# Value products of a windowed attention: both halves of the values side by side in 64 columns, the sums of the exponentials on VectorE, the division on GpSimd

## The chip, the cores and the metric

The kernel runs on one core of one Trainium2 chip. A core has five engines with a queue each[...]: TensorE (PE, with its weight loads shown as PEld), VectorE (DVE), ScalarE (ACT), GpSimd (POOL) and SyncE (SP), which here only issues transfers. What counts is the device time of one execution in microseconds; smaller is better. With one core there is no other core to wait for.

## The reference, cut to what matters

The program is one transformer block of the macaron kind on 4096 tokens of 256 features: half a mixture-of-experts feed-forward, then attention in windows of 64 tokens, then another half feed-forward with the same weights. The change touches the attention alone, and of it the softmax and the product with the values:

```python
xg = x.reshape(Bx, ng, LS, Cx)                 # windows of LS = 64 tokens, H = 16 heads of hd = 16
qkv = jnp.einsum('bglc,cd->bgld', xg, w_qkv)
q, k, v = jnp.split(qkv, 3, axis=-1)
...
att = jnp.einsum('bghqd,bghkd->bghqk', q, k) * scale
att = jnp.where(causal, att, -jnp.finfo(att.dtype).max)
att = jax.nn.softmax(att, axis=-1)
y = jnp.einsum('bghqk,bghkd->bghqd', att, v)
...
x = x + 0.5 * _L0_ffn_ref(_layernorm(x, axis=-1), ...)
x = x + _L0_attn_ref(_layernorm(x, axis=-1), ...)
x = x + 0.5 * _L0_ffn_ref(_layernorm(x, axis=-1), ...)
```

The feed-forward is a shared one (`silu(x @ sg) * (x @ su) @ sd`, 2048 wide) plus the two best of 8 experts for each token, each expert taking at most 640 tokens.

## The kernel before

Matrix products are made in fp16 with each operand split in a high part and a low part (the rounding error of the high one). A product of two split operands is three matmuls, high by high, high by low and low by high (`TERMS`, L35); a value that is already exact in one place needs two.

There are four phases (L747 to L785). In phase a the first shared feed-forward runs for half of the tokens while 32 tiles of 128 tokens are normalised and routed to the experts. Phase b is the first round of experts. In phase c the rest of the first shared feed-forward and most of the second one are the main work, and beside them 32 attention tiles of 128 tokens run. Phase d is the second round of experts and the last shared block. The change lies wholly in phase c.

Main work of phase c: `shared` (L345) handles a block of 512 tokens in 16 chunks of 128 hidden features. A chunk is `gate_up` (L292): six 128x512 matmuls for the gate into one PSUM tile `pgu`, a tanh on ACT (L309), a multiplication on DVE (L310), six matmuls for the up part into another `pgu`, a product on DVE (L315), the rounding to the high part `hh` on ACT (L317) and the low part `hl` on DVE (L318). Then `down` (L321) puts twelve 128x256 matmuls into the two accumulators `po`; it is deferred by one chunk, so that the PE has the next chunk's gate and up to do meanwhile. There are three PSUM buffers for `pgu`. One is free again when L310 or L315 has read it, so a late DVE instruction shows as a PE that waits for `DVE sl L310`. At the end of a block two more DVE instructions (L359) add the result to the residual.

Side work of phase c: `attn_tile` (L469) is a generator; each `yield` ends a step. `drive` (L673) lets the main work advance and gives the side work a share: with `RATE_C = 3` every live tile advances by one step for each chunk of the main work, and with `GAP_C = 4` a new tile starts every four chunks. So four tiles go with one block of 512 tokens, and within one chunk several tiles are at different steps: the tile that makes its maximum (L545) and copies its values (L550) stands beside its predecessor that makes its value products (L568).

The steps of a tile that matter here: the scores of 16 heads come from `psc` (L537, eight 128x64 matmuls for each of two windows `g`), and DVE adds the causal mask into `S`, [128, 16, 64] (L540). DVE takes the maximum over the keys (L545), POOL subtracts it (L546), and ACT copies the values `vs` into `V2` four times (L550). One step later ACT takes the exponential in place (L554) and rounds it to fp16 into `e16` (L556), and POOL makes the low part (L557). One step later a transposing DMA turns both into `ET`, [128, 16, 128], whose partitions hold high and low parts of the 64 keys. Two steps later come the value products:

- For every pair of heads the stationary operand is `ET` (128x128) and the moving one is 33 columns of `V2`: two heads' 16 features and a column of ones, whose product is the sum of the exponentials. There are two matmuls into the same columns of `py`, one for the high part of the values and one for the low part (L568, 32 matmuls a tile).
- DVE takes the reciprocal of the sums out of `py` (L571, once for each `g`), and multiplies `py` by it into `Y` (L574, twice for each `g`, 64 partitions each).

In the next step ACT rounds `Y` to fp16 (L162) and POOL makes the low part (L163); transposing DMAs, the output projection and the front of the second feed-forward follow (`front_steps`, L602; `stats`, L134, with its power on POOL, L142; `route`, L209; `scatter`, L275, with two indirect DMAs for each tile on POOL's queue, L283). For one tile out of four, POOL's queue has the scatters of a whole block of 512 tokens beside its attention work.

The order of the instructions on each engine's queue is fixed when the program is built. The builder goes by the order of the code and by a model of the time that each instruction takes (L821), so instructions of one engine that don't depend on each other may change places. [...]

```python
    with _tile.TileContext(nc, schedule_with_timeline_sim=True) as tc:
```

Of the kernel before, what the change touches and what calls it, by code (L numbers as in the profile page):

```python
# [8 lines left out]
F32 = mybir.dt.float32  # L9
F32R = mybir.dt.float32r  # L10
F16 = mybir.dt.float16
# [4 lines left out]
ALU = mybir.AluOpType  # L16
AX = mybir.AxisListType
# [3 lines left out]
P = 128  # L21
# [16 lines left out]
class Net:  # L38
# [395 lines left out]
    def attn_init(self, w_qkv, ln_w, w_proj):  # L434
        nc = self.nc
        a = self.at
        self.wqkv = a.tile([P, 2, 2, 3 * H], F16, name="wqkv")
        self.wpr = a.tile([P, 2, 2, H], F16, name="wpr")
        for k in range(2):
            for c0, n in ((0, 2 * H), (2 * H, H)):  # L440
                r = a.tile([P, 2 * H], F32, name="rq", tag="q32")[:, :n]
                nc.sync.dma_start(out=r, in_=w_qkv[k * P:(k + 1) * P, c0:c0 + n])
                self.split(self.wqkv[:, 0, k, c0:c0 + n], self.wqkv[:, 1, k, c0:c0 + n], r)
        wp = w_proj.rearrange("(j r c) f -> r j c f", r=2, c=16)
        for k in range(2):
            r = a.tile([P, H], F32, name="rp", tag="yy")
            for j in range(8):
                nc.sync.dma_start(out=r[j * 16:(j + 1) * 16], in_=wp[k, j])
            self.split(self.wpr[:, 0, k], self.wpr[:, 1, k], r)
        self.lnw = a.tile([P, H], F32, name="lnw")  # L450
        nc.sync.dma_start(out=self.lnw, in_=ln_w.unsqueeze(0).to_broadcast([P, H]))
        self.mask = a.tile([P, 64], F32, name="mask")
        m2 = self.sm.tile([P, 64], F32, name="m2", bufs=1)
        for m, base in ((self.mask, 0), (m2, -64)):
            nc.gpsimd.memset(m, 0.0)
            nc.gpsimd.affine_select(
                out=m, in_=m, pattern=[[-1, 64]], compare_op=ALU.is_ge, fill=-3.0e38,
                base=base, channel_multiplier=1)
        nc.vector.tensor_copy(self.mask[64:P], m2[64:P])
        self.QK = a.tile([P, 24, P], F16, name="QK")  # L460
        nc.gpsimd.memset(self.QK, 0.0)
        self.V2 = []
        for i in range(2):
            v = a.tile([P, 2, 2, 8, 34], F16, name=f"V2{i}")
            nc.gpsimd.memset(v[:, :, 0, :, 32:33], 1.0)
            nc.gpsimd.memset(v[:, :, 1, :, 32:33], 0.0)
            self.V2.append(v)

    def attn_tile(self, R, j, x2, new_fb):  # L469

        nc = self.nc
        a = self.at
# [11 lines left out]
        V2 = self.V2[j % 2]  # L484
# [8 lines left out]
        for i in range(2):  # L493
            nc.scalar.activation(qk[:, i, :], pqk[:, i, :], AF.Square, scale=1.0 / XP, accum_out=ss[:, i:i + 1])
        nc.vector.tensor_scalar(
            out=ss, in0=ss, scalar1=XP ** 2 / H, scalar2=1e-6 * XP ** 2, op0=ALU.mult, op1=ALU.add)
# [6 lines left out]
            out=vs[:, 1, :], in0=pv, scalar=1.0 / XP, in1=vs[:, 0, :], op0=ALU.mult, op1=ALU.subtract)  # L503
        yield
        yield
        for i in range(2):
            nc.vector.scalar_tensor_tensor(
                out=qk[:, i, :], in0=pqk[:, i, :], scalar=ss[:, i:i + 1], in1=self.lnw,
                op0=ALU.mult, op1=ALU.mult)
        QS = self.QK[:, 0:16].rearrange("p (j s) (r a c) -> p j s r a c", s=2, r=2, a=4)  # L510
        for i in range(2):
            if i == 0:
                for r in range(2):
# [5 lines left out]
                        out=s[:, :, 2:4, :], in0=src, in1=s[:, :, 0:2, :], op=ALU.subtract)  # L519
            else:  # L520
# [4 lines left out]
                    out=s[:, :, 1::2, :], in0=src, in1=s[:, :, 0::2, :], op=ALU.subtract)  # L525
        yield
        QT = a.tile([P, 2, 24, 64], F16, name="QT")
        for g in range(2):
            nc.sync.dma_start_transpose(
                out=QT[:, g], in_=self.QK[g * 64:(g + 1) * 64].rearrange("p j c -> p (j c)"))  # L530
        yield
        yield
        S = a.tile([P, 16, 64], F32, name="S")
        for g in range(2):
            p = self.m1([P, 8, 64], F32, "psc")
            for jj in range(8):
                nc.tensor.matmul(  # L537
                    p[:, jj, :], lhsT=QT[:, g, 2 * jj:2 * jj + 2, :].rearrange("p r q -> p (r q)"),
                    rhs=QT[:, g, 16 + jj, :], start=True, stop=True)
            nc.vector.tensor_tensor(  # L540
                out=S[:, g * 8:(g + 1) * 8, :], in0=p,
                in1=self.mask.unsqueeze(1).to_broadcast([P, 8, 64]), op=ALU.add)
# [4 lines left out]
            out=S, in0=S, in1=mx.unsqueeze(2).to_broadcast([P, 16, 64]), op=ALU.subtract)  # L547
        for g in range(2):
            for d in range(2):
                nc.scalar.copy(  # L550
                    V2[d * 64:(d + 1) * 64, g, :, :, 0:32],
                    vs[g * 64:(g + 1) * 64].rearrange("p l (j c) -> p l j c", c=32))
        yield
        nc.scalar.activation(S, S, AF.Exp, scale=0.25)  # L554
        e16 = a.tile([P, 16, 2, 64], F16, name="e16")
        nc.scalar.copy(e16[:, :, 0, :], S)  # L556
        self.anchor = nc.gpsimd.tensor_tensor(out=e16[:, :, 1, :], in0=S, in1=e16[:, :, 0, :], op=ALU.subtract)  # L557
        yield
        ET = a.tile([P, 16, P], F16, name="ET")
# [2 lines left out]
        yield  # L562
        Y = a.tile([P, 2, 8, 16], F32, name="Y", tag="yy")
        for g in range(2):
            py = self.m1([P, 8, 33], F32, "py")
            for jj in range(8):
                for l in range(2):
                    nc.tensor.matmul(  # L568
                        py[:, jj, :], lhsT=ET[:, g * 8 + jj, :], rhs=V2[:, g, l, jj, 0:33], start=(l == 0), stop=(l == 1))
            rc = self.sm.tile([P, 8], F32, name="rc")  # L570
            nc.vector.reciprocal(rc, py[:, :, 32])  # L571
            for r in range(2):
                sl = slice(r * 64, (r + 1) * 64)
                nc.vector.tensor_tensor(  # L574
                    out=Y[sl, g], in0=py[sl, :, r * 16:(r + 1) * 16],
                    in1=rc[sl].unsqueeze(2).to_broadcast([64, 8, 16]), op=ALU.mult)
        yield
        y = self.tok.tile([P, H], F32, name="y")
        nc.sync.dma_start(out=y, in_=R["acc"][j * P:(j + 1) * P])
# [246 lines left out]
```

## Time and profile before

| what | us |
|---|---|
| median of 3 runs | 1846.73 (1844.07 to 1847.13) |
| the profiled execution, its own time | 1844.18 |
| its span, first to last instruction | 1842.5 |
| first and last value product (L568) | 698.3 and 1317.8 |

| engine | 1020 to 1080 us, busy of 60.00 us | whole span, busy |
|---|---|---|
| PE | 59.34 | 1782.8 |
| DVE | 48.85 | 1204.9 |
| ACT | 40.03 | 952.2 |
| POOL | 40.69 | 769.5 |

The stretch from 1020 to 1080 us lies in the middle of phase c. A busy share tells how loaded an engine is and not which one sets the time; for that one looks at the few places where the PE waits, and follows the chain of releases back from there. The granted TensorE clock was 0.999 of full speed over the span, so the clock plays no part.

### The profile page before, as it was taken

To read this page: it belongs to the slowest core of one execution; us is meant where nothing else is said; L and a number is where in the kernel's file an instruction comes from. 1 tells how busy PE (TensorE), PEld (TensorE's weight loads), DVE (VectorE), ACT (ScalarE), POOL (GpSimd) and SP (SyncE) were. 2 spreads that over 40 slices of the span, in tenths; PEclk is the share of its full clock that TensorE was granted. 3 is DMA by queue.
4 is the path that set the end of the run, shared out by engine and by line. 5 is a ranking of instruction groups with operands and counts; after the bars stand their busy time and mean duration, and the time that the engine had idled before them with its cause. 6 is when DMAs were issued, how large, how long until landed. Compare 5 with 4: busy or idle time off the path is not lost.

```text
span 1842.5 us, 37619 instructions
## 1 busy us (share of the span) xinstructions
PE 1782.8 (97%) x13722; PEld 1197.0 (65%) x13722; DVE 1204.9 (65%) x2869; ACT 952.2 (52%) x2055; POOL 769.5 (42%) x1104
## 2 busy tenths in 40 slices
PE   6989999999999899999999999999999999999999
PEld 3545656777777556666666666666665677777765
DVE  7665545666666567787877878787755565666643
ACT  5333324555555365766666666666333455555542
POOL 7776540111221244567667676776530011112210
PEclk9999999999999999999999999999999999999999
DMA  9753022445554246767585776757213044455420
GB/s 291 224 142 94 12 63 69 107 107 114 128 115 101 58 80 110 118 114 158 104 148 117 140 137 119 152 98 125 48 30 87 27 111 111 108 112 127 104 47 12
DMA packets 447514, 196.61 MB, mean 107 GB/s; under 512 B 302369, under 2 KB 444381, under 8 KB 447264
## 3 DMA queue, kind: packets, MB, share of 16 engines
q1 hardware_dynamic: 429664, 173.03, 42.7%
q0 software_dynamic: 17664, 21.17, 6.7%
q8 instruction: 107, 1.75, 0.4%
q14 instruction: 79, 0.65, 0.1%
HBM read 81.04 MB, written 52.85 MB: 73 GB/s over the span
## 4 chain that ended last, share of the span: by engine, by line
PE 57%; POOL 12%; issue 11%; DVE 10%; DMA 5%; ACT 4%; SPq 1%; POOLq 0%; DVEq 0%; another core or an unknown queue 0%; ACTq 0%
PE pgu L302 36%; PE po L326 18%; POOL xg L283 3%; DVE sl L315 2%; DVE sl L310 1%; POOL X L281 1%; DVE hl L318 1%; POOL rstd L142 1%; POOL S L546 1%; DMA y<-in_L_attn_x_dram 1%; ACT hh L317 1%; PE pqk L599 1%; ACT sl L309 1%; POOL e L557 1%; DMA xg<-X,di 1%
## 5 line engine op out<-in xcount | busy, mean ns | idle before, releaser
L302 PE MATMUL pgu<-xb,sgu 128*128 128x512 f16 x3072 | 743.5, 380 | 20.3 <-DVE sl L310 8.0
L317 ACT CAST hh<-sl 128x512 f16<-128x512 f32 (+2 forms) x512 | 272.9, 533 | 485.4 <-DVE sl L315 471.4
L302 PE MATMUL pgu<-xe,wc 128*128 128x384 f16 (+1 forms) x3072 | 497.0, 299 | 0.8
L302 PEld LDWEIGHTS <-sgu 128*128 128x128 f16 x3072 | 294.0, 98 | 295.7 <-issue 29.6
L315 DVE SCALAR_TENSOR_TENSOR sl<-pgu,sl 128x512 f32<-128x512 f32 (+2 forms) x512 | 300.6, 587 | 215.5 <-PE pgu L302 180.1
L318 DVE TENSOR_TENSOR hl<-sl,hh 128x512 f16<-128x512 f32 (+2 forms) x512 | 311.0, 608 | 160.1 <-ACT hh L317 153.3
L326 PEld LDWEIGHTS <-hh 128*128 128x128 f16 x3328 | 319.8, 98 | 114.9 <-ACT hh L317 13.9
L302 PEld LDWEIGHTS <-wc 128*128 128x128 f16 x3072 | 300.5, 98 | 94.1 <-issue 1.9
L326 PE MATMUL po<-sdw,hh 128*128 128x256 f16 x2048 | 349.9, 273 | 10.1 <-ACT hh L317 6.8
L326 PE MATMUL po<-sdw,hl 128*128 128x256 f16 x1024 | 247.5, 273 | 11.7 <-DVE hl L318 10.4
L326 PE MATMUL po<-wd,hh 128*128 128x256 f16 x1280 | 223.6, 273 | 0.0
L326 PEld LDWEIGHTS <-hl 128*128 128x128 f16 x1664 | 162.8, 98 | 57.2 <-DVE hl L318 23.3
L422 POOL DMA_INDIRECT out_dram<-eo,eid x40 | 64.1, 1604 | 314.3 <-DVE hl L318 244.9
L313 ACT ACTIVATE sl<-pgu 128x384 f32<-128x384 f32 (+1 forms) x336 | 158.9, 473 | 56.7 <-PE pgu L302 27.6
L422 POOL DMA_INDIRECT acc<-eo,eid x40 | 64.8, 1621 | 266.2 <-DVE hl L318 227.4
L283 POOL DMA_INDIRECT xg<-X,di x128 | 131.3, 1026 | 66.2 <-issue 27.5
L326 PE MATMUL po<-wd,hl 128*128 128x256 f16 x640 | 152.5, 273 | 2.1 <-DVE hl L318 1.9
L310 DVE SCALAR_TENSOR_TENSOR sl<-sl,pgu 128x512 f32<-128x512 f32 x176 | 120.0, 682 | 45.4 <-ACT sl L309 43.2
L309 ACT ACTIVATE sl<-pgu 128x512 f32<-128x512 f32 x176 | 104.3, 593 | 42.3 <-PE pgu L302 36.3
L102 ACT ACTIVATE wc<-re 128x512 f16<-128x512 f32 x128 | 80.5, 629 | 78.0 <-PE pgu L302 51.2
L103 DVE SCALAR_TENSOR_TENSOR wc<-re,wc 128x512 f16<-128x512 f32 x128 | 88.3, 690 | 25.9 <-ACT wc L102 25.7
L546 POOL TENSOR_TENSOR S<-S,amx 128x1024 f32<-128x1024 f32 x32 | 62.1, 1939 | 79.1 <-DVE amx L545 72.1
(141 smaller groups left out, 1740.6 us busy)
## 6 DMA issues: line engine op xcount, KB each, us to landing
re<-in_L_ffn_rg_dram SPq DMA_DIRECT2D x128, 128.0 KB
re<-in_L_ffn_ru_dram SPq DMA_DIRECT2D x128, 128.0 KB
re<-in_L_ffn_rd_dram SPq DMA_DIRECT2D x128, 128.0 KB
xg<-zero SPq DMA_DIRECT2D x16, 650.0 KB
y<-acc SPq DMA_DIRECT2D x64, 128.0 KB
y<-in_L_attn_x_dram SPq DMA_DIRECT2D x32, 128.0 KB
acc<-xr SPq DMA_DIRECT2D x16, 256.0 KB
out_dram<-xr SPq DMA_DIRECT2D x16, 256.0 KB
```

The source lines that it names most:

```text
L103: nc.vector.scalar_tensor_tensor(out=lo, in0=src, scalar=WS, in1=hi, op0=ALU.mult, op1=ALU.subtract)
L283: i = nc.gpsimd.indirect_dma_start(out=R["xg"][:, :], out_offset=bass.IndirectOffsetOnAxis(ap=di[:, t, k:k + 1], axis=0), in_=X, in_offset ...
L302: nc.tensor.matmul(p, lhsT=wc[:, w, i, k, :], rhs=x[:, 2 * a + k, :], start=(j == 0), stop=(j == 5))
L309: nc.scalar.activation(s, p, AF.Tanh, scale=0.5 / XP)
L310: nc.vector.scalar_tensor_tensor(out=s, in0=s, scalar=1.0, in1=p, op0=ALU.add, op1=ALU.mult)
L313: nc.scalar.activation(s, p, AF.Silu, scale=1.0 / XP)
L315: nc.vector.scalar_tensor_tensor(out=s, in0=ps[1], scalar=1.0 / XP / (2.0 * XP if tanh else 1.0), in1=s, op0=ALU.mult, op1=ALU.mult)
L317: nc.scalar.copy(h[0], s)
L318: nc.vector.tensor_tensor(out=h[1], in0=s, in1=h[0], op=ALU.subtract)
L326: nc.tensor.matmul(o, lhsT=h[a][:, t * P:(t + 1) * P], rhs=wd[:, w], start=(c == 0 and j == 0 and t % 2 == 0), stop=(c == nch - 1 and j == 2),
L422: i = nc.gpsimd.indirect_dma_start(out=R["acc"][:, :], out_offset=bass.IndirectOffsetOnAxis(ap=ids[:, t:t + 1], axis=0), in_=eo, in_offset ...
L546: self.anchor = nc.gpsimd.tensor_tensor(out=S, in0=S, in1=mx.unsqueeze(2).to_broadcast([P, 16, 64]), op=ALU.subtract)
```

## The change

`V2` becomes [128, 2, 8, 2, 32]: for each pair of heads the high part's 32 columns and the low part's 32 columns lie side by side, and the column of ones is gone. One matmul with 64 moving columns takes the place of the two with 33. The sums of the exponentials come from a new reduction of `S` on VectorE (128 partitions, 16 heads of 64 keys), made in the step of the exponential, with one reciprocal for all 16 heads. VectorE adds the high and the low product out of `py`, a reduction over two elements, twice for each `g`. GpSimd then multiplies `Y` in place by the reciprocal, once for each `g`. The exponential that is summed is the fp32 one, where before it was the sum of its two fp16 parts.

```diff
-            v = a.tile([P, 2, 2, 8, 34], F16, name=f"V2{i}")
-            nc.gpsimd.memset(v[:, :, 0, :, 32:33], 1.0)
-            nc.gpsimd.memset(v[:, :, 1, :, 32:33], 0.0)
-            self.V2.append(v)
+            self.V2.append(a.tile([P, 2, 8, 2, 32], F16, name=f"V2{i}"))
...
-                    V2[d * 64:(d + 1) * 64, g, :, :, 0:32],
+                    V2[d * 64:(d + 1) * 64, g].rearrange("p j l c -> p l j c"),
                     vs[g * 64:(g + 1) * 64].rearrange("p l (j c) -> p l j c", c=32))
         yield
         nc.scalar.activation(S, S, AF.Exp, scale=0.25)
         e16 = a.tile([P, 16, 2, 64], F16, name="e16")
         nc.scalar.copy(e16[:, :, 0, :], S)
+        rc = self.sm.tile([P, 16], F32, name="rc")
+        nc.vector.tensor_reduce(out=rc, in_=S, axis=AX.X, op=ALU.add)
+        nc.vector.reciprocal(rc, rc)
         self.anchor = nc.gpsimd.tensor_tensor(out=e16[:, :, 1, :], in0=S, in1=e16[:, :, 0, :], op=ALU.subtract)
...
-            py = self.m1([P, 8, 33], F32, "py")
+            py = self.m1([P, 8, 2, 32], F32, "py")
             for jj in range(8):
-                for l in range(2):
-                    nc.tensor.matmul(
-                        py[:, jj, :], lhsT=ET[:, g * 8 + jj, :], rhs=V2[:, g, l, jj, 0:33], start=(l == 0), stop=(l == 1))
-            rc = self.sm.tile([P, 8], F32, name="rc")
-            nc.vector.reciprocal(rc, py[:, :, 32])
+                nc.tensor.matmul(
+                    py[:, jj].rearrange("p l c -> p (l c)"), lhsT=ET[:, g * 8 + jj, :],
+                    rhs=V2[:, g, jj].rearrange("p l c -> p (l c)"), start=True, stop=True)
             for r in range(2):
                 sl = slice(r * 64, (r + 1) * 64)
-                nc.vector.tensor_tensor(
-                    out=Y[sl, g], in0=py[sl, :, r * 16:(r + 1) * 16],
-                    in1=rc[sl].unsqueeze(2).to_broadcast([64, 8, 16]), op=ALU.mult)
+                cs = slice(r * 16, (r + 1) * 16)
+                nc.vector.tensor_reduce(
+                    out=Y[sl, g], in_=py[sl, :, :, cs].rearrange("p j l c -> p j c l"), axis=AX.X, op=ALU.add)
+            nc.gpsimd.tensor_tensor(
+                out=Y[:, g], in0=Y[:, g], in1=rc[:, g * 8:(g + 1) * 8].unsqueeze(2).to_broadcast([P, 8, 16]),
+                op=ALU.mult)
```

## The prediction

> **What bounds the kernel now.** I read the page first, then the groups of instructions between 660 and 1325 us with shapes kept apart, then the PE's timeline for its waits, then the chain of waits, and last the timelines of POOL and DVE. The page:
>
> ```profile
> span 1842.5 us, 37619 instructions
> PE 1782.8 (97%) x13722; PEld 1197.0 (65%) x13722; DVE 1204.9 (65%) x2869; ACT 952.2 (52%) x2055; POOL 769.5 (42%) x1104
> ```
>
> The PE is busy 97% of the span, which says that saved PE work could pay, not that it does. The durations of the operations that the change removes, or that are the nearest rows to what it adds (columns: line, engine, operation, tile, shapes, count, then busy us and mean ns of one):
>
> ```profile
> L568 PE MATMUL py<-V,ET 128*128 128x33 f16 x1024 | 31.1, 177 | 0.0
> L537 PE MATMUL psc<-QT 128*128 128x64 f16 x512 | 28.4, 193 | 0.0
> L571 DVE RECIPROCAL rc<-py 128x8 f32<-128x8 f32 x64 | 10.0, 184 | 2.1 <-remote 1.8
> L574 DVE TENSOR_TENSOR Y<-py,rc 64x128 f32<-64x128 f32 x128 | 36.6, 286 | 1.6
> L545 DVE TENSOR_REDUCE amx<-S 128x16 f32<-128x1024 f32 x32 | 38.8, 1211 | 0.1
> L518 POOL TENSOR_TENSOR QK<-qk,QK 128x256 f16<-128x256 f32 x62 | 41.0, 682 | 11.4 <-ACT QK L517 11.4
> ```
>
> The last row is the nearest to the new POOL work: 682 ns for 256 elements a partition. Matmuls overlap, so 177 and 193 ns are not what one costs. The chain of waits, between 690 and 760 us, has their pace (start, us, what):
>
> ```profile
> 714.22 0.47 PE psc L537 x16
> 738.07 0.80 PE py L568 x32
> ```
>
> 0.80/32 is 25.0 ns for a matmul of 33 columns, 0.47/16 is 29.4 ns for one of 64. Next, where the PE waits in the middle of phase c (its timeline; in brackets the idle time ahead and what ended it):
>
> ```profile
> 1017.47 1.46 PE L302 MATMUL pgu<-xb,sgu 128*128 128x512 f16 x6 [0.87 <-DVE sl L310]
> 1018.76 0.96 PE L568 MATMUL py<-V,ET 128*128 128x33 f16 x32
> 1019.57 0.38 PE L326 MATMUL po<-sdw,hh 128*128 128x256 f16 x2
> 1020.66 0.28 PE L326 MATMUL po<-sdw,hl 128*128 128x256 f16 x1 [0.71 <-DVE hl L318]
> ```
>
> This pair of waits comes back at 855.69, 936.79, 1098.16, 1178.86 and 1259.56 us: six times, once in 80.7 us, which is one block of 512 tokens with four attention tiles. Between them the PE runs without a gap (but 0.26 us at 918). So each of these six blocks ends with the PE waiting for DVE, and the PE alone isn't the bound. The chain of waits from 995 to 1080 us tells where the late DVE instruction comes from:
>
> ```profile
> 1041.56 1.29 PE pgu L302 x6
> 1043.04 0.90 issue
> 1043.94 0.39 ACT yp L162
> 1044.33 0.50 ACT sl L309
> 1044.85 0.69 DVE sl L310
> ...
> 1047.00 1.04 DVE dl L226
> 1048.41 0.55 POOL rstd L142
> ...
> 1059.16 1.13 DVE amx L545
> ```
>
> From 1042.85 (the end of the first piece) to the wait at 1098.16, which is 55.3 us, no PE work is on it: it goes through ACT, DVE and POOL. After 1066.5 it is mostly POOL, whose queue holds the scatters of the block (its timeline, in the last of the four tiles):
>
> ```profile
> 1083.80 1.10 POOL L283 DMA_INDIRECT xg<-X,di  x1 [0.31 <-issue]
> 1084.90 1.93 POOL L546 TENSOR_TENSOR S<-S,amx 128x1024 f32<-128x1024 f32 x1
> 1087.00 0.99 POOL L283 DMA_INDIRECT xg<-X,di  x1 [0.17 <-POOL S L546]
> ```
>
> POOL has no wait over 0.32 us between 1066.5 and 1093.1. So two things are within 1.6 us of each other in 80.7: the PE's own work, and a chain over the three other engines, and the longer is the chain.
>
> [...] 1211 ns for 1024 elements and 205 ns for 64 (L259) make 1.05 ns an element and 138 ns fixed; no row shows a reduction out of PSUM. [...] hl (L318, two SBUF inputs) takes 689 ns on average between 60 and 660 us and 760 ns in phase c, where POOL works beside it.
>
> **The change part by part, for one tile.**
>
> PE: 32 matmuls at 25.0 ns go and 16 at 29.4 come, 0.80 - 0.47 = -0.33 us. Over 32 tiles 10.6 us, if the PE sets the time throughout.
>
> DVE, the value step: two reciprocals of 0.20 and four multiplications that follow at 0.30 (1.20 for the four) go, 1.6 us. Four reductions of 64x256 into 64x128 come: 138 + 256 x 1.05 = 0.41 us each by the reduction row, 0.34 from start to start, since independent DVE instructions overlap by 0.08 (the 1.21 us of L545 is followed after 1.13). That is 1.4 to 1.6 us. [...] PSUM with the stride of 32 could add, and I bound it at twice, 3.2. I take 1.5: no change here. DVE adds no wait, it still waits for py.
>
> DVE, the exponential step, all new: a reduction just like L545 (1.13 us to the next instruction) and a reciprocal of 128x16 (0.20, as L571), 1.33 us. It waits for the exponential on ACT, and behind it in DVE's queue are that chunk's L310, L315 and L318, for which the PE's `pgu` buffers wait. Four tiles of a block, four places. (1) At 1024.87, the exponential's end, DVE is idle for 0.82 us and the PE is ahead on its own: hidden. (2) At 1044.04 DVE is idle until y (L592, 1044.34) and L310 at 1044.85; the reduction runs 1044.1 to 1045.2 and pushes a stretch that has no gap until 1048.4, where POOL's rstd (1048.41) waits for its end. With the gap used up, 0.95 us is left, on the chain. It stays there: POOL is then without a gap up to its ss at 1053.66, and DVE from 1054.4 to 1060.3. (3) At 1064.59 DVE is full too, but what follows on the chain is POOL, which gets to its rstd at 1072.27 while DVE has delivered the input (L140) at 1069.5: 2.8 us of cover, so hidden. (4) At 1087.93 the same: L140 ends at 1089.5, rstd starts at 1092.01. Without the cover each costs up to 1.33.
>
> POOL, all new: two multiplications of 128x128. From 682 ns at 256 elements and 1902 at 1024 (L546) it is 1.59 ns an element and 0.28 fixed, so 0.48 us each; start to start POOL's rows overlap by 0.06, so 0.42. Bounds: 0.2 (its smallest rows, L215) and 0.68. For tiles 1 to 3 POOL is waiting anyway around its yp (idle 1.46, 2.87 and 2.72 us ahead of it). In tile 4 it isn't: 0.84 us, all on the chain. Four memsets (L465, L466), 3.1 us of POOL at 630 us, go; the chain there is a scatter's DMA and weight loads, so nothing.
>
> ACT: the V2 copies have the same 64x512 elements, 0.62 us each. The rounding of Y (L162) now waits for POOL instead of DVE. Behind it in ACT's queue is the tanh (L309), for which L310 and the PE wait. For tiles 1 and 2 the multiplication is done in time, as L162 stands behind the exponential there. In tile 4 it isn't sure: at 1002.68 L162 starts as soon as Y is there, but POOL is in its scatters and in S until 1006.15. If the multiplication is queued behind S, L162 starts at 1007.0 and the tanh moves from 1002.99 to 1007.4; the up matmuls at 1006.2 need that chunk's L310, which then ends at 1008.7. A PE stall of 2.5 us, of which the 0.87 + 0.95 + 0.84 that the PE waits at the block's end anyway would take most: 0 to 2.5 us. I take 0.
>
> Sum for one of the six blocks: +0.95 + 0.84, and of the PE's gain only the one product that lies in the PE's part of the chain (1039.44), -0.33: +1.46. The saved PE time of the other products makes the wait at the block's end longer, that is what is late next: L310 behind POOL. Six blocks: +8.8. The other 8 tiles (before 830 and after 1263 us, where the chain is PE work or the PE has no such wait): 8 x -0.33 = -2.6. Together +6.2, from 1844.2 to 1850.4 for the profiled execution; its 1844.18 is 2.6 below the median of 1846.73, so 1852.9 against that.
>
> **The rivals.** *B, the whole PE gain:* the order of each queue is made anew when the program is built, and the reduction and the divisions may fall in gaps; the waits at the ends of blocks stay at 1.6 us. 10.6 off, 1836. For it: PE busy 59.34 of 60, DVE has 11 us of 60 idle. Against: with PE work gone, nothing shortens the POOL stretch. It decides if added DVE and POOL work costs the chain under 0.3 us a block. *C, everything added is hidden, and the gain goes into the wait at the block's end:* (8 + 6) x 0.33 = 4.6, 1842. Against it: POOL's stretch from 1066 to 1093. *D, queues behind a waiting head:* forecast plus the 2.5 us of tile 4 undiminished, 6 x 2.5 = 15 more: 1868. For it: ACT already idles 2.54 us at 1006.18 behind POOL's S. Against it: the overlap with the wait at the block's end.
>
> **How the numbers follow.** Forecast 0.42 (1853), B 0.22, C 0.16, D 0.20. The range takes B's centre and D's: 1836 to 1868, which leaves half of each, 0.2, outside. 0.2% is 3.7 us, about what a measurement of this kernel can tell from no change. Faster: B, 0.10 of C, 0.02 of the forecast where tile 2's reduction finds a gap: 0.34. Slower: D and 0.26 of the forecast: 0.46. The rest, 0.20, within.
>
> **What would show it.** PE: L568 with 512 matmuls, 0.47 us for 16. DVE: L545's twin at 1.21 us, the reductions out of py near 0.41. The wait of the PE for L310 at the end of each block grows from 0.87 to about 3, and the period from 80.7 to 82. If the period falls to 79.4, B is right; if tanh stands behind yp while POOL is in S, D. I am wrong if the blocks' order of instructions changes so that the POOL stretch isn't ahead of the PE's wait, or if a reduction out of PSUM costs far over 0.41.

## The result and the profile after

The changed kernel takes 1855.38 us (median of 7 runs, 1850.58 to 1859.45) against 1846.73 before (7 runs, 1844.07 to 1851.62). The ratio is 1.0047, with a 95% interval of 1.0032 to 1.0063: slower, by about 9 us. The profiled execution took 1859.45 us, with a span of 1857.7; it is the slowest of the seven, so the traces are compared by their periods and not by their ends. Line numbers are from here on those of each run's own kernel: the subtraction of the maximum on GpSimd is L546 before and L543 after.

The page of the changed kernel, busy times and shares of the chain of waits, and under it the second of these lines for the kernel before:

```profile
PE 1781.0 (96%) x13210; PEld 1188.3 (64%) x13210; DVE 1271.9 (68%) x2869; ACT 944.9 (51%) x2055; POOL 803.6 (43%) x1164
...
PE 59%; DVE 15%; issue 9%; DMA 5%; POOL 5%; ACT 5%; SPq 1%; another core or an unknown queue 0%; DVEq 0%; POOLq 0%; ACTq 0%
```

```profile
PE 57%; POOL 12%; issue 11%; DVE 10%; DMA 5%; ACT 4%; SPq 1%; POOLq 0%; DVEq 0%; another core or an unknown queue 0%; ACTq 0%
```

VectorE (DVE) is 67 us busier than before, GpSimd (POOL) 34. On the chain VectorE has gone from 10% to 15%, and GpSimd from 12% to 5%, although GpSimd has more to do: what the end hangs on has moved to VectorE. The groups of the changed kernel between 660 and 1355 us (line, engine, operation, tile, shapes, count, busy us, mean ns of one, idle time ahead):

```profile
L573 DVE TENSOR_REDUCE Y<-py 64x128 f32<-64x256 f32 x128 | 53.7, 419 | 1.8
L555 DVE TENSOR_REDUCE rc<-S 128x16 f32<-128x1024 f32 x32 | 38.8, 1212 | 6.3 <-ACT S L551 6.0
L575 POOL TENSOR_TENSOR Y<-Y,rc 128x128 f32<-128x128 f32 x64 | 27.8, 444 | 23.6 <-DVE Y L573 22.7 <-DMA QT<-QK 0.8
L567 PE MATMUL py<-V,ET 128*128 128x64 f16 x512 | 21.9, 193 | 0.0
L556 DVE RECIPROCAL rc<-rc 128x16 f32<-128x16 f32 x32 | 7.7, 241 | 0.1
```

The new instructions have about the lengths that were expected. Two old ones have not kept theirs. They are hl (L318), the low part of the feed-forward's hidden features, and nm (L150), minus the mean times the inverse deviation of each token, made twice for each tile. Both in the middle of phase c (840 to 1260 us), before and then after:

```profile
L318 DVE TENSOR_TENSOR hl<-sl,hh 128x512 f16<-128x512 f32 x83 | 61.1, 736 | 18.5 <-ACT hh L317 15.7 <-ACT S L554 1.4
L150 DVE SCALAR_TENSOR_TENSOR nm<-amv,arstd 128x1 f32<-128x1 f32 x21 | 3.2, 154 | 2.2 <-POOL arstd L142 2.2
```

```profile
L318 DVE TENSOR_TENSOR hl<-sl,hh 128x512 f16<-128x512 f32 x81 | 70.7, 873 | 17.5 <-ACT hh L317 13.7 <-issue 3.8
L150 DVE SCALAR_TENSOR_TENSOR nm<-amv,arstd 128x1 f32<-128x1 f32 x20 | 16.0, 798 | 1.6 <-POOL arstd L142 1.1
```

So hl takes 873 ns on average where it took 736, and one of the two nm, which has a single element a partition, 798 ns instead of 154. The waits of the PE in one block of the changed kernel:

```profile
1014.69 0.28 PE L326 MATMUL po<-sdw,hl 128*128 128x256 f16 x1 [0.84 <-DVE hl L318]
1020.84 0.61 PE L326 MATMUL po<-sdw,hh 128*128 128x256 f16 x4 [1.41 <-ACT hh L317]
1024.57 1.45 PE L302 MATMUL pgu<-xb,sgu 128*128 128x512 f16 x6 [0.72 <-DVE sl L310]
1042.74 0.39 PE L326 MATMUL po<-sdw,hh 128*128 128x256 f16 x2 [0.93 <-ACT hh L317]
1043.96 0.28 PE L326 MATMUL po<-sdw,hl 128*128 128x256 f16 x1 [0.82 <-DVE hl L318]
```

Where the PE waited 1.58 us in a block of 80.69 us, it now waits 4.7 us in this block and 4.3 in the median one, of 82.9 us (a block is counted from one POOL subtraction of S to the fourth after it). Its busy time in a block has fallen from 79.1 to 78.5 us, which is less than the 1.3 us that four tiles at 0.33 would give; where the rest went the trace doesn't show.

The timelines show why old instructions have grown. First VectorE, then GpSimd, in the changed kernel:

```profile
1017.18 2.16 DVE L150 SCALAR_TENSOR_TENSOR nm<-amv,arstd 128x1 f32<-128x1 f32 x1
...
1034.59 1.91 DVE L318 TENSOR_TENSOR hl<-sl,hh 128x512 f16<-128x512 f32 x1
```

```profile
1017.20 2.11 POOL L557 TENSOR_TENSOR e<-S,e 128x1024 f16<-128x1024 f32 x1
...
1033.82 2.13 POOL L557 TENSOR_TENSOR e<-S,e 128x1024 f16<-128x1024 f32 x1 [0.27 <-ACT e L553]
```

The GpSimd instruction beside both is e, the low part of the exponentials. The nm with one element ends when e ends (1019.34 and 1019.31). The hl begins 0.77 us into its e and ends 0.55 us after it (1036.50 and 1035.95). Both VectorE instructions have two tensor inputs in SBUF. From 840 to 1260 us, 26 of the 81 hl took over 0.73 us, up to 2.94, and each of the 26 ended 0.54 to 0.61 us after a GpSimd instruction did. The products sl (L310, L315) have as many elements, but one of their inputs is in PSUM: of these 163, 42 began inside a GpSimd instruction that wrote e, S, QK, yp, X, xa or Y and had up to 1.6 us left, and none took over 0.693 us. Nor did any of the new reductions of S, with one SBUF input, take over 1.221 us; 5 of the 20 began inside one, with up to 0.6 us left. Two inputs in SBUF aren't the whole of it, as ss (L492), with one tensor input, once took 0.66 us where 0.15 is its median, and ended 0.03 us after a GpSimd instruction. So the traces show VectorE instructions held until a GpSimd instruction ends; by what, they don't show. For nm and e they don't tell which began first either, as the two records start 0.02 us apart. While VectorE stands there, what is queued behind it stands too: L315, the next after this nm, starts at 1019.26.

### The profile page after: what moved, and what is told of

It is laid out like the page before. It is cut to its first block, busy times and chain, and to the rows that moved or that the text cites. A ratio compares the mean times of both kernels' runs of the same rounds, so it can differ in the third digit from the quotient of the medians.

```text
span 1857.7 us, 36680 instructions
## 1 busy us (share of the span) xinstructions
PE 1781.0 (96%) x13210; PEld 1188.3 (64%) x13210; DVE 1271.9 (68%) x2869; ACT 944.9 (51%) x2055; POOL 803.6 (43%) x1164
## 4 chain that ended last, share of the span: by engine, by line
PE 59%; DVE 15%; issue 9%; DMA 5%; POOL 5%; ACT 5%; SPq 1%; another core or an unknown queue 0%; DVEq 0%; POOLq 0%; ACTq 0%
PE pgu L302 37%; PE po L326 19%; DVE hl L318 3%; DVE sl L315 2%; DVE sl L310 2%; ACT hh L317 1%; POOL xg L283 1%; DVE Y L573 1%; PE pqk L600 1%; DMA xg<-X,di 1%; ACT V L547 1%; DVE nm L150 1%; DVE rc L555 1%; DMA xb<-X 1%; DVE st L137 1%
## 5 line engine op out<-in xcount | busy, mean ns | idle before, releaser
L315 DVE SCALAR_TENSOR_TENSOR sl<-pgu,sl 128x512 f32<-128x512 f32 (+2 forms) x512 | 300.3, 587 | 209.8 <-PE pgu L302 179.3
L318 DVE TENSOR_TENSOR hl<-sl,hh 128x512 f16<-128x512 f32 (+2 forms) x512 | 322.8, 631 | 149.6 <-ACT hh L317 141.5
L310 DVE SCALAR_TENSOR_TENSOR sl<-sl,pgu 128x512 f32<-128x512 f32 x176 | 119.0, 676 | 35.2 <-ACT sl L309 34.1
L543 POOL TENSOR_TENSOR S<-S,amx 128x1024 f32<-128x1024 f32 x32 | 62.1, 1940 | 74.6 <-DVE amx L542 74.6
```

The source lines that it names most:

```text
L310: nc.vector.scalar_tensor_tensor(out=s, in0=s, scalar=1.0, in1=p, op0=ALU.add, op1=ALU.mult)
L315: nc.vector.scalar_tensor_tensor(out=s, in0=ps[1], scalar=1.0 / XP / (2.0 * XP if tanh else 1.0), in1=s, op0=ALU.mult, op1=ALU.mult)
L318: nc.vector.tensor_tensor(out=h[1], in0=s, in1=h[0], op=ALU.subtract)
```

## The experiments

Three theories were set against each other. *VectorE work*: the reductions as such fill its queue. *GpSimd*: the divisions lengthen its stretch with the scatters. *Port*: the lost time is VectorE instructions with two SBUF inputs waiting for a GpSimd instruction to end. Port is only its name in the expectations; no run shows where the two engines meet. A fourth says that the builder only put the queues in a worse *order*. Every edit makes the builder order all queues anew, so one small ratio alone proves little. Ratios are to executions of the kernel before that were made beside each run, with 95% intervals. Names that start with a_ are edits of the changed kernel, those with b_ edits of the kernel before.

| run | ratio | interval | median us | block us | hl ns |
|---|---|---|---|---|---|
| before | 1 | | 1842.83 to 1844.40 beside these runs | 80.69 | 736 |
| the change | 1.0047 | 1.0032 to 1.0063 | 1855.38 | 82.89 | 873 |
| a_nosum | 1.0014 | 1.0007 to 1.0020 | 1846.28 | 81.74 | 918 |
| a_nodiv | 0.9991 | 0.9982 to 0.9999 | 1841.97 | 80.71 | 795 |
| a_neither | 0.9964 | 0.9950 to 0.9978 | 1838.04 | 80.30 | 882 |
| b_halfpe | 0.9932 | 0.9915 to 0.9949 | 1831.43 | 79.30 | 733 |
| b_plus_sum | 1.0013 | 1.0006 to 1.0019 | 1845.12 | 81.31 | 899 |
| b_plus_div | 1.0022 | 1.0012 to 1.0032 | 1847.25 | 81.24 | 814 |
| a_divdve | 1.0125 | 1.0109 to 1.0142 | 1866.49 | 86.50 | 941 |
| a_nm | 1.0022 | 1.0013 to 1.0031 | 1847.34 | 81.62 | 884 |
| a_psum | 0.9985 | 0.9976 to 0.9993 | 1842.33 | 80.19 | 685 |
| b_psum | 0.9998 | 0.9990 to 1.0007 | 1843.62 | 79.83 | 684 |
| a_code | 1.1102 | 1.1085 to 1.1119 | 2047.33 | | 717 |
| b_code | 1.1092 | 1.1075 to 1.1109 | 2046.95 | | 730 |

The last two columns are from one profile each: the median period of a block, and the mean length of hl from 840 to 1260 us.

**The clock.** One thing has to be known before these ratios are read. In the profile of the changed kernel, after its longest wait of the PE, the granted TensorE clock was 0.50 from 855.8 to 859.2 us:

```profile
854.74 0.61 PE L326 MATMUL po<-sdw,hh 128*128 128x256 f16 x4 [2.13 <-ACT hh L317]
```

```profile
855.80:859.20 3.40, 3.40 (x20) 2.09 (x19) 2.79 (x8) 1.92 (x5) 2.14 (x4) 0.50 0.93 165
```

The second line lists the stretch, the busy time of PE, PEld, DVE, ACT and POOL, the clock, and the share and rate of the transfers. Such stretches of 3.41 us at half the clock occur between 660 and 1355 us in three of the twelve profiles in the builder's timed order: once here, four times in a_nosum, three times in a_divdve. All eight begin 0.3 to 1.3 us after the end of a wait of 2.06 to 2.66 us; four other waits of 2.47 to 2.65 us had none behind them, and no shorter wait had one. Each takes 1.7 us of PE time (half of 3.41). The profile of the kernel before has none in phase c. In the three runs they come to 1.7, 6.8 and 5.1 us.

**What is the PE's time worth?** Half of the value matmuls are left out of the kernel before:

```diff
-                for l in range(2):
+                for l in range(1):
                     nc.tensor.matmul(
-                        py[:, jj, :], lhsT=ET[:, g * 8 + jj, :], rhs=V2[:, g, l, jj, 0:33], start=(l == 0), stop=(l == 1))
+                        py[:, jj, :], lhsT=ET[:, g * 8 + jj, :], rhs=V2[:, g, l, jj, 0:33], start=True, stop=True)
```

> Leaves out the product with the low part of the values: the kernel before with 16 value matmuls of 33 columns a tile instead of 32, everything else as it was. It takes 0.40 us a tile from the PE, 12.8 us over 32 tiles. If the PE's own work sets the time: 1833 to 1836. By the prediction's reading (a chain over the other engines is 1.6 us a block longer than the PE's work): about 14 tiles' worth, 5.6 us, so 1841.

It gained 12.2 us (1843.67 to 1831.43), or 12.5 by the ratio, of the 12.8 taken away. So the PE's time was worth nearly all of its length, and not less than half of it as the prediction had read from the chain. The PE's waits in one block of this run:

```profile
1014.99 0.28 PE L326 MATMUL po<-sdw,hl 128*128 128x256 f16 x1 [1.11 <-DVE hl L318]
1073.52 0.28 PE L326 MATMUL po<-sdw,hl 128*128 128x256 f16 x1 [0.34 <-DVE hl L318]
```

They are 1.45 us a block, no longer than before (1.58): the chain over the other engines, which looked as long as the PE's, drew in with it. Here the queues have an order of their own too, so it isn't shown whether the chain followed the PE or the new order made it shorter.

**Parts of the change taken away.** Without the sum (the division then multiplies by a tile `rone` that is filled with a constant once at the start; that line is left out here):

```diff
-        rc = self.sm.tile([P, 16], F32, name="rc")
-        nc.vector.tensor_reduce(out=rc, in_=S, axis=AX.X, op=ALU.add)
-        nc.vector.reciprocal(rc, rc)
+        rc = self.rone
```

> Leaves out the sum of the exponentials: the changed kernel without the reduction of S on VectorE and its reciprocal; the division multiplies by a constant tile instead. VectorE theory (the added VectorE work, 1.45 us a tile, sets the period of a block): the PE's saving comes through, 1836 to 1843 us, and the block period falls from 83 to about 80. GpSimd theory (the division in GpSimd's scatter stretch sets it): still slow, 1850 to 1856. Order theory (the new order of the queues costs, not the work): no fixed value, the waits of the PE stay at 4 to 5 us a block.

Without the division:

```diff
-            nc.gpsimd.tensor_tensor(
-                out=Y[:, g], in0=Y[:, g], in1=rc[:, g * 8:(g + 1) * 8].unsqueeze(2).to_broadcast([P, 8, 16]),
-                op=ALU.mult)
```

> Leaves out the division: the changed kernel without GpSimd's two multiplications a tile; the sums and reciprocals are still made. VectorE theory: still slow, 1850 to 1856, since VectorE has the same work. GpSimd theory: 1840 to 1846, six blocks less 0.9 us of GpSimd and less waiting of ScalarE behind it. Order theory: anywhere.

Without both:

> Leaves out both the sum and the division; what is left of the change are the 64-column matmuls and the reductions out of the PSUM tile. All the PE's saving (10.6 us) and no added work but 0.1 us of VectorE a tile: 1834 to 1840 us by the VectorE and the GpSimd theory; near 1847 or above by the order theory, or if the PE's saving is worth nothing.

Taking away the sum brought the ratio down by 0.33%, the division by 0.56%, both by 0.83%. VectorE's theory missed with the first (1836 to 1843 expected) and with the second (still slow expected); GpSimd's met the second and missed the first. The first miss decides less than it seems to. The run without the sum had a mean granted clock of 0.994 over its 20 executions, against 0.998 of the kernel before beside it, and its profile lost 6.8 us of PE time to half-clock stretches; without them it would stand near 1839.5, an estimate from its 1846.3, and inside VectorE's range. Both additions cost. And what is left without them, 0.9964, is 6.6 us of the 10.6 that the PE saves; the new reductions out of PSUM are in it. Waits for GpSimd remain even without the sum (hl takes 918 ns on average), and the six PE waits of 2.6 us in that run each end on one; VectorE and then GpSimd:

```profile
1078.87 3.17 DVE L318 TENSOR_TENSOR hl<-sl,hh 128x512 f16<-128x512 f32 x1
```

```profile
1079.09 1.28 POOL L517 TENSOR_TENSOR QK<-qk,QK 128x256 f16<-128x256 f32 x2
1080.34 1.15 POOL L523 TENSOR_TENSOR QK<-qk,QK 128x512 f16<-128x512 f32 x1
```

The hl stood behind three GpSimd instructions in a row, until 0.55 us after the last of them ended (1082.04 and 1081.49), and the PE waited for it:

```profile
1082.10 0.28 PE L326 MATMUL po<-sdw,hl 128*128 128x256 f16 x1 [2.65 <-DVE hl L318]
```

**Parts of the change added alone to the kernel before.** The reduction and the reciprocal as in the change, into a tile that nobody reads:

> The kernel before plus the reduction of S on VectorE and its reciprocal, whose result is not used. VectorE theory (added VectorE work as such): about 0.95 us in each of six blocks as predicted, up to the 6 us that leaving it out of the changed kernel gave: 1849 to 1853 against a before of 1846.7, a ratio of 1.001 to 1.0035. Port theory (the time goes where VectorE instructions with two SBUF inputs wait for a GpSimd instruction to end; the reduction has one input): a ratio within 0.002 of 1, unless the new order of the queues makes hl (L318) longer.

The two multiplications after each Y, by a tile of ones that is made once at the start:

```diff
                     in1=rc[sl].unsqueeze(2).to_broadcast([64, 8, 16]), op=ALU.mult)
+            nc.gpsimd.tensor_tensor(
+                out=Y[:, g], in0=Y[:, g], in1=self.rone[:, g * 8:(g + 1) * 8].unsqueeze(2).to_broadcast([P, 8, 16]),
+                op=ALU.mult)
```

> The kernel before plus the two GpSimd multiplications a tile, by a tile of ones, between Y and its rounding. GpSimd theory: 0.9 us in each of six blocks and what ScalarE loses behind it, a ratio of 1.003 to 1.006. Port theory: the same sign, but with hl (L318) and nm (L150) longer than before (736 and 154 ns in the middle of phase c). If neither the ratio nor these two grow, the division alone isn't what costs in the changed kernel.

By the ratios they cost 2.4 and 4.1 us. The reduction costs a twentieth of its 46 us of work, the division a seventh of its 28. Singly they explain less than the change loses: -10.6 for the PE, 4.0 for what a_neither fell short of that, 2.4 and 4.1 make about zero, and +8.7 was measured. The rest comes only when they are together, or with the order that the builder then chose. Nor are these prices free of waits for GpSimd: with the sum added hl grew from 736 to 899 ns, with the division to 814.

**How full is VectorE's queue?** The division on VectorE instead of GpSimd:

```diff
-            nc.gpsimd.tensor_tensor(
+            nc.vector.tensor_tensor(
                 out=Y[:, g], in0=Y[:, g], in1=rc[:, g * 8:(g + 1) * 8].unsqueeze(2).to_broadcast([P, 8, 16]),
```

> The changed kernel with the division on VectorE instead of GpSimd: two multiplications of 128x128 a tile, about 0.29 us each, 0.5 us a tile more for VectorE and 0.9 less for GpSimd. GpSimd or port theory: faster than the changed kernel, a ratio to before of 0.998 to 1.003. VectorE theory: slower than the changed kernel, 1.005 to 1.009.

GpSimd's theory, and the port theory as I had put it, fail here: this is the slowest of the kernels in the builder's timed order. VectorE got two instructions of 0.283 us a tile, 2.3 us in a block; they have two SBUF inputs too, but in the middle of phase c none took over 0.293 us, so they weren't held. The block grew by 3.6 us at the median and by 2.5 averaged over five blocks, 0.7 of these through the lower clock. In the changed kernel VectorE time was thus paid for nearly in full; VectorE's theory has the sign, and its 1.005 to 1.009 was too small.

**The waits of hl and nm for GpSimd taken away.** First nm, with one input as a scalar of each partition:

```diff
-            nc.vector.scalar_tensor_tensor(
-                out=nm, in0=mv[:, 0:1], scalar=-1.0, in1=rstd, op0=ALU.mult, op1=ALU.mult)
+            nc.vector.tensor_scalar(
+                out=nm, in0=mv[:, 0:1], scalar1=rstd, scalar2=-1.0, op0=ALU.mult, op1=ALU.mult)
```

> The changed kernel with the product of mean and rstd (L150) as a tensor_scalar, one tensor input and the other as a scalar operand of each partition, so that it is no longer an instruction with two SBUF tensor inputs; the work is the same, and little of the queues' order changes. Port theory: L150 falls from 798 and 241 ns to about 150, VectorE gains up to 0.6 us a tile, and the ratio to before falls from 1.0047 to 1.001 to 1.003. VectorE-work and GpSimd theories: no change, 1.004 to 1.006.

Then hl too, whose first input stays in PSUM:

```diff
+        u = ps[1] if tanh else s
         nc.vector.scalar_tensor_tensor(
-            out=s, in0=ps[1], scalar=1.0 / XP / (2.0 * XP if tanh else 1.0), in1=s, op0=ALU.mult, op1=ALU.mult)
-        nc.scalar.copy(h[0], s)
-        nc.vector.tensor_tensor(out=h[1], in0=s, in1=h[0], op=ALU.subtract)
+            out=u, in0=ps[1], scalar=1.0 / XP / (2.0 * XP if tanh else 1.0), in1=s, op0=ALU.mult, op1=ALU.mult)
+        nc.scalar.copy(h[0], u)
+        nc.vector.tensor_tensor(out=h[1], in0=u, in1=h[0], op=ALU.subtract)
```

> The changed kernel with both kinds of waiting VectorE instructions rewritten to one SBUF tensor input: nm (L150) as in the run before, and in phase c the product of gate and up stays in its PSUM tile, so that hl takes one operand from PSUM and one from SBUF. The work is the same. Port theory: hl falls from 873 to about 690 ns in the middle of phase c, VectorE gains some 1 us a tile more, and the PE's saving comes through at last: a ratio to before of 0.993 to 0.999. VectorE-work and GpSimd theories: hl's length was only a symptom, ratio 1.001 to 1.004 as with nm alone.

And both in the kernel before; the two runs with both rewrites differ by the change without these waits:

> The kernel before with the same two rewrites. In it hl takes 736 ns and nm 154 in the middle of phase c, so there is little waiting to take away: a ratio of 0.996 to 1.000 by the port theory. [...] the port theory has the changed one ahead, the VectorE-work and GpSimd theories have this one ahead by 0.2 to 0.4%.

The groups of the first run with both rewrites, 840 to 1260 us:

```profile
L319 DVE TENSOR_TENSOR hl<-pgu,hh 128x512 f16<-128x512 f32 x84 | 57.5, 685 | 14.3 <-ACT hh L318 13.1
L318 ACT CAST hh<-pgu 128x512 f16<-128x512 f32 x84 | 49.0, 584 | 67.3 <-DVE pgu L316 66.1
L150 DVE TENSOR_SCALAR nm<-amv,arstd 128x1 f32<-128x1 f32 x21 | 4.3, 207 | 1.9 <-POOL arstd L142 1.9
```

The rewritten nm takes 207 ns and hl 685, with as much work as before. The changed kernel went from 1.0047 to 1.0022 with nm, and to 0.9985 with both; 0.62% in all, 11 us. By the mean clock of the executions, 0.997 with the change and 0.999 with nm rewritten, up to 3 of the first 4.6 us may be the clock (an estimate); with both rewrites the mean is 0.998. The kernel before as a whole gained nothing that could be measured (0.9998). ScalarE's rounding (hh) also became 31 ns shorter out of PSUM, 584 ns where it took 615; the kernel before has that too, so it isn't what sets the two apart.

The step with nm is the cleanest experiment here, because the order hardly changed. In the five blocks from the eighth to the 28th subtraction of S, 782 of VectorE's 810 instructions stand in the same order as in the changed kernel, 548 of ScalarE's 559, 438 of GpSimd's 440 and 2956 of the PE's 3060. These blocks fell from 414.0 to 407.4 us. Of these 6.6 us, 1.7 are the half-clock stretch, which this run doesn't have: its longest PE wait there is 1.61 us. The step with hl isn't so clean, as only 511 of the 810 keep their order.

The kernel before did gain in these five blocks: they fell from 403.9 to 398.4 us. It lost that again elsewhere, 6.8 us of it ahead of them. The changed kernel's fell from 414.0 to 401.9. So in these blocks the change costs 10.1 us with the waits of hl and nm for GpSimd and 3.5 us without them, and the waits are about two thirds of the loss. The PE's waits between 830 and 1270 us agree: 9.8 us in the kernel before and 22.6 after the change, 3.6 and 11.3 with both rewrites. By the whole time the waits are more than the loss, and without them the change is level with the kernel before or 0.13% ahead (0.9985 against 0.9998; the intervals overlap). Either way these waits are the larger part, and the added work on VectorE and GpSimd takes most of the PE's 0.6%. The changed kernel with both rewrites is faster than either kernel of the case.

**The order of the queues.** Both kernels in the order of the code:

```diff
-    with _tile.TileContext(nc, schedule_with_timeline_sim=True) as tc:
+    with _tile.TileContext(nc, schedule_with_timeline_sim=False) as tc:
```

> The changed kernel with its queues in the order of the code, without the builder's model of time. To be read against the kernel before in the same order. Order theory (the change loses because the queues were put in another order): in the order of the code the change wins, by up to the PE's 10 us. Port, VectorE-work and GpSimd theories: it loses here too, or gains less than 2 us, since the added work is the same.

> The kernel before with its queues in the order of the code. Slower than before by an amount that no theory gives, since the model of time is there to fill gaps; it is the base for the changed kernel in the same order.

The ratios are 1.1102 and 1.1092, with intervals that overlap. The change doesn't win in the other order either, so a bad draw of the order alone isn't needed to explain that it brings no gain. But these kernels are 200 us slower, their PE is busy 89 and 90% of the span, their granted clock is 0.97, and hl is short in both (717 and 730), so this says little about the tight case.

## Why the prediction was right, point by point

- **Sign and size.** 1853 was forecast, 1855.4 measured; 6.2 us slower forecast, 8.7 measured. The sum held better than its reading: two of its steps were off, in opposite directions, so the closeness is in part luck.
- **The PE's saving a tile** held: the 16 new matmuls are 0.63 us from the first start to the last end, and (0.63 - 0.193)/15 is 29 ns from one to the next.
- **"The PE alone isn't the bound", and its saved time mostly lengthens the wait at the block's end:** this failed. Half the value matmuls gone gave 12.5 of 12.8 us, so rival B's premise was right for the PE alone. The chain of 55 us over the other engines was real in that trace, but with less PE work, and the order that came with it, it was shorter. That those engines only keep step with the PE's queue is the likely reason; no run shows it.
- **The value step on VectorE** was taken as equal, at 1.5 us for the four reductions; they take 1.74 from first start to last end, 419 ns each. That is within 12 ns of the 407 reckoned from the reductions out of SBUF (138 + 256 x 1.05), so the PSUM source and the stride of 32 cost next to nothing.
- **The reduction of S,** 1.21 and 0.24 us, held as work. Its price of 0.95 us a block was too high for the addition alone: 2.4 us over six blocks are 0.4. Taken out of the changed kernel it gave back 0.33%, which is 1.0 a block, with a lower clock against it.
- **The division on GpSimd,** 0.444 us where 0.48 was taken, priced at 0.84 us a block: the addition alone cost 4.1/6 = 0.7. Held for the addition; taken out of the changed kernel it gave back 0.56%, 1.7 a block.
- **What is late next:** "L310 behind POOL", a wait that grows from 0.87 to about 3 us. The PE's wait in a block grew by about 3 us (1.58 to 4.3 in the median block), but before hh, hl and L310 at three to five places, and GpSimd's share of the chain fell. The period was to be 82 and is 82.9.
- **The missing term:** VectorE instructions with two SBUF inputs that stand behind GpSimd instructions. The prediction named the longer hl, 760 ns in phase c where it took 689 before, and gave the wait no price. By the two rewrites it is 11 us of the whole time, and 6.6 of the 10.1 us that the change costs in five blocks. It worked against the PE step, which had counted too little of the saving (4.6 of 10.6 us), and so the sum came out near. The half clock after long waits, 1.7 us in the profile, had no term either.
- **Rival D** (ScalarE's rounding of Y in front of the tanh behind GpSimd's S) isn't seen: at 1015.28 us of the changed kernel's scatter tile that rounding (L162) comes after the tanh (1013.60), and from 830 to 1260 us ScalarE waits for the division ahead of that rounding only once, for 0.16 us.

What stays open: which of several hl that wait for GpSimd hurts. The kernel with neither sum nor division has an hl of 882 ns and is fast, so a long mean alone doesn't make a kernel slow; that it costs only where the PE has no slack for it is the likely reading. Only the rewritten nm and the division added alone (790 of VectorE's 810 instructions in the same order) nearly held the builder's order; every other run carries a new one. Why the kernel before lost outside the middle of phase c what the rewrites gave it there is open, and so is whether the long wait itself brings the half clock: the traces show only that the one came ahead of the other.

## What to carry to other kernels

Where the PE's work and a chain over the other engines are within 2% of each other, as here, don't count a saving on the PE at its full length if work is put on the others: price the added work at more than zero even where each instruction seems to have a gap. Before moving work to GpSimd, look for VectorE instructions with two SBUF tensor inputs in the same stretch, and try an operand in PSUM or as a scalar of each partition (here hl fell from 873 to 685 ns and nm from 798 to 207); measure it, as the kernel before gained nothing by it on the whole (0.9998). A chain of waits that runs beside a PE without gaps isn't proof that the PE is free; take PE work away and see. And look at the granted clock of every run before a small difference is explained.

## What was not expected of the hardware

An instruction of one element a partition (nm), with two SBUF tensor inputs, took up to 2.16 us while a GpSimd instruction of 2.11 us was running, and 0.80 on average; rewritten with one input as a per-partition scalar it takes 0.21. Without the sum, an hl was held over three GpSimd instructions in a row, 3.17 us against 0.69, although its record begins 0.22 us before the first of them, while small GpSimd copies ran: the waiting VectorE instruction didn't get in between. The subtraction itself isn't faster with one operand in PSUM: at the median it takes 0.692 us in the kernel before and 0.691 with the rewrite; the averages, 0.736 and 0.685, differ by those that were held (15 of the 83 took over 0.73 us in the kernel before). And after a wait of the PE of 2.06 to 2.66 us the granted clock fell to 0.50 for 3.41 us in eight of twelve cases.
